# A Mamba block with two feed-forward blocks on one core: state products in halves, sums a tick sooner, carried states in the first factors, four residual additions a unit on GpSimd

## The chip, the core and the metric

The kernel runs on one core of a Trainium2 chip. Its engines are TensorE (PE in the profile; its weight loads PEld), VectorE (DVE), ScalarE (ACT), GpSimd (POOL) and SyncE (SP), which issues nearly all transfers. Each engine works through a queue of its own in order and waits on semaphores for the others. The metric is the device time of one execution in microseconds, as the median over the runs; one further execution is recorded by the hardware profiler.

## The reference

Input `x` is (4, 1024, 256) in fp32. All arithmetic is fp32.

```python
def block(x):
    x = x + attn(layernorm(x))
    return x + ffn(layernorm(x))

def attn(u):                       # Mamba, then a gated MLP, each with an RMS norm
    h = u + mamba(rmsnorm(u, norm1_w))
    xn = rmsnorm(h, norm2_w)
    return h + (silu(xn @ gate_w.T) * (xn @ up_w.T)) @ down_w.T      # 704 wide

def mamba(u):
    z, x, B, C, dt_raw = split(u @ in_proj_w.T)
    dt = softplus(dt_raw @ dt_proj_w.T + dt_proj_b)
    # 8 groups x 32 channels p, each with 32 states n; over the sequence t:
    #   h[t] = exp(dt[t] * A) * h[t-1] + dt[t] * x[t] * B[t];  y[t] = sum_n h[t] * C[t]
    y = scan(x, dt, A, B, C) + x * D_param
    return (y * silu(z)) @ out_proj_w.T

def ffn(x):                        # 1024 wide, with a Walsh-Hadamard transform
    return fwht(silu(x @ W1.T) * (x @ W3.T)) @ W2.T
```

The scan is the large part: 256 channels with 32 states, 4 sequences of 1024 steps.

## The kernel before, in words

**Units.** A unit is half a sequence, T = 512 steps: `c` = 0 the first half (even units), `c` = 1 the second (odd units), eight units in order. Tokens are the free dimension in the scan.

**Quads and ticks.** The 256 x 32 states of a unit are 64 blocks of 128 partitions (32 states for 4 channels) x 512 steps. Four blocks make a quad, 16 quads a unit, 128 in all. A quad takes two ticks, so a unit has 32 and the kernel 256. Quad q belongs to ticks 2q and 2q+1:

- `dma_da` (L693) spreads dt from DRAM over the state partitions into the tile `da` [128, 4, 512] (1 MB); four such buffers (`pda`). `dma_ub` (L698) does the same with dt*x, half a quad at a time (six buffers), `dma_cr` (L711) with C for two quads.
- `exp` (L720) on ScalarE turns `da` into exp(dt*A), two blocks a tick, a quad ahead.
- `times_b` (L740) on VectorE makes `bx` = dt*x*B in PSUM, two blocks a tick; `scan` (L753) runs two scans a tick on VectorE, `da` in place: each step multiplies by `da` and adds `bx`. Where `c` = 1, the initial value is a per-partition operand, the state that the first half left in the tile `carry`.
- `times_c` (L760) on GpSimd, once per quad in the even tick after it, copies the last states of the four blocks to `carry` where `c` = 0, and multiplies the whole quad by C (L768).
- `sum_states` (L772) on TensorE, in the odd tick after that, adds over the states with four matmuls into `py`, over eight quads. Then a buffer of `da` is free. After the eighth quad `y_dx` (L791, VectorE, tick 2q+4) adds x*D, and `y_z` (L798, GpSimd, tick 2q+5) multiplies by silu(z).

**The dense work** is placed in ticks by hand: `at(tick, lane, fn)` puts a function in a list, and the loop at the end (L840 to L876) runs every tick's lanes in a fixed order (PE, ACT, the scan's steps, DVE, POOL0, `times_c`, POOL, `sum_states`, PEend, ACTend, SP, the reads, SPend). That order is each engine's queue; nothing reorders it later. `pre(u, H)` (L324) norms a unit, transposes it and projects it for its scan, which starts at tick H = 32k; `post(u, E, other)` (L590) does out_proj, the MLP and the FFN of a unit after its scan, E = 32k + 32. So during a unit's scan the engines also do the `post` of the unit before, the end of the one before that, and the `pre` of the next.

In `post`, `add_rows` (L296) does a matmul from tokens back to model columns, two row tiles per PSUM tile, and adds the result to the residual tile `hr` on VectorE between the two scans of a tick (L316). It is called for out_proj (tick E+3, addition at E+4), for the MLP's down projection (E+18) and for W2 (E+36, additions at E+38 and E+40). `row_stats` and `hn` on ScalarE, small vectors on GpSimd (L195, L333 and others) and transposes on TensorE make each norm. `gated` (L245) does the two gated projections: TensorE in steps, silu and a PSUM copy `up` on ScalarE, the product on GpSimd (L274).

**SyncE's queue** holds all reads of the scan in the order of the ticks: at an odd tick `dma_da(q+3)`, after the sums of quad q-1 that free its buffer, then `dma_cr(q+2)`; `dma_ub` six ticks ahead.

Of the kernel before, what the change touches and what calls it, by code (L numbers as in the profile page):

```python
# [9 lines left out]
F32 = mybir.dt.float32  # L10
AF = mybir.ActivationFunctionType
ALU = mybir.AluOpType
# [3 lines left out]
P = 128  # L16
# [3 lines left out]
T = 512  # L20
# [7 lines left out]
def tile_block(ctx: ExitStack, tc: tile.TileContext, a, out):  # L28
# [20 lines left out]
    nc = tc.nc  # L49
# [4 lines left out]
    p3 = ctx.enter_context(tc.tile_pool(name="p3", bufs=3))  # L54
# [10 lines left out]
    def dense_psum():  # L65
        return ps_m.tile([P, T], F32, tag="dense", name="dense")
# [14 lines left out]
    us = [{"b": b, "c": c} for b in range(BATCH) for c in range(SEQ // T)]  # L81
# [80 lines left out]
    def row_stats(u, src, ts, centred=True):  # L162

        if 0 in ts:
            u["mv"] = sm.tile([P, 2, TT], F32, tag="mv", name="mv")
        for t in ts:
            junk = p1.tile([P, DM], F32, tag="junk", name="junk")
            nm, ms = u["mv"][:, 0, t : t + 1], u["mv"][:, 1, t : t + 1]
            if centred:
                nc.scalar.activation(  # L170
                    junk, src[:, t, :], AF.Identity, scale=-1.0 / (16 * DM), accum_out=nm
                )
            nc.scalar.activation(  # L173
                junk,
                src[:, t, :],
                AF.Square,
                bias=nm if centred else 0.0,
                scale=1.0 / 16,
                accum_out=ms,
            )  # L180
# [57 lines left out]
    def at(tick, lane, fn, *args):  # L238
        todo[tick][lane].append(partial(fn, *args))

    def run(tick, lane):
        for fn in todo[tick].pop(lane, ()):
            fn()
# [49 lines left out]
        for i in range(1, len(chunks)):  # L293
            at(tick + 3, "POOL", product, i)

    def add_rows(tick, u, lhs, rhs, per_tick, lane="PE"):  # L296

        po = {}

        def pe(t):  # L300
            if t % 2 == 0:
                po[t // 2] = dense_psum().rearrange("p (t d) -> p t d", t=2)
            left, right = lhs(), rhs()
            n = len(left)
            for k in range(n):
                nc.tensor.matmul(  # L306
                    po[t // 2][:, t % 2, :],
                    lhsT=left[k][:, t * P : (t + 1) * P],
                    rhs=right[k],
                    start=(k == 0),  # L310
                    stop=(k == n - 1),
                )

        def add(i):
            hr = u["hr"][:, 2 * i : 2 * i + 2, :]
            nc.vector.tensor_tensor(hr, hr, po[i], ALU.add)  # L316

        for t in range(TT):
            at(tick + t // per_tick, lane, pe, t)
            if t % 2:  # L320
                at(tick + t // per_tick + 1, "DVE", add, t // 2)


    def pre(u, H):  # L324

        s = {}
# [227 lines left out]
        else:  # L554
# [6 lines left out]
            at(H - 31, "ACT", un, (2, 3))  # L561
            at(H - 30, "PE", lambda: transposes(u, s["un"]))
            at(H - 30, "ACTend", transposed, u, "ut")
        at(H - 24, "PE", pe_x)
        at(H - 23, "ACT", act_x)
        at(H - 22, "SP", dma_xb)
        at(H - 19, "SPend", dma_xr, 0)
        at(H - 17, "SPend", dma_xr, 1)
        at(H - 16, "PE", pe_dt)
# [20 lines left out]
    def post(u, E, other):  # L590


        s = {}
# [28 lines left out]
        def store():  # L622
# [11 lines left out]
            lambda: [W["wo"][:, k, :] for k in range(2)],  # L634
            4,
            "PEend",
        )
        at(E + 5, "ACTend", lambda: row_stats(u, u["hr"], (0, 1), False))
        at(E + 6, "ACTend", lambda: row_stats(u, u["hr"], (2, 3), False))
# [26 lines left out]
        for i in range(3):  # L666
# [4 lines left out]
            lambda: [u["g"][:, c, :] for c in range(8)],  # L671
            lambda: [w2h[:, c, :] for c in range(8)],
            1,
        )
        at(E + 43, "SPend", store)

# [3 lines left out]
    qs = [  # L680
        {"u": us[q // 16], "h": q // 8 % 2, "j": q // 2 % 4, "g": q % 2, "n": q % 16}
        for q in range(NQ)
    ]
# [9 lines left out]
    def dma_da(q):  # L693
        s = qs[q]
        s["da"] = pda.tile([P, 4, T], F32, tag="da", name="da")
        spread(s, s["da"], "dtd")
# [35 lines left out]
    def carry_of(s):  # L732
        return s["u"]["carry"][:, s["h"], s["j"], :, s["g"]]
# [19 lines left out]
    def scan(q, b):  # L753
        s = qs[q]
        u = s["u"]
        da = s["da"][:, b, :]
        start = 0.0 if u["c"] == 0 else carry_of(s)[:, b : b + 1]
        nc.vector.tensor_tensor_scan(da, da, s["bx"][:, b % 2, :], start, ALU.mult, ALU.add)  # L758

    def times_c(q):  # L760
        s = qs[q]
        u = s["u"]
        if u["c"] == 0:
            if s["n"] == 0:
                kept = p2.tile([P, 2, 4, 4, 2], F32, tag="carry", name="carry")
                u["carry"] = us[us.index(u) + 1]["carry"] = kept
            nc.gpsimd.tensor_copy(carry_of(s), s["da"][:, :, T - 1])  # L767
        nc.gpsimd.tensor_tensor(  # L768
            s["da"], s["da"], s["cr"].unsqueeze(1).broadcast_to([P, 4, T]), ALU.mult
        )  # L770

    def sum_states(q):  # L772
        s = qs[q]
        u = s["u"]
        first, last = s["n"] % 8 == 0, s["n"] % 8 == 7
        if first:
            u["py"] = ps_y.tile([P, T], F32, tag="y", name="py")
        for b in range(4):
            nc.tensor.matmul(  # L779
                u["py"][32 * b : 32 * b + 32, :],  # L780
                lhsT=rsel[:, 2 * s["j"] + s["g"], :],
                rhs=s["da"][:, b, :],
                start=first,
                stop=last,
            )
        if last:
            at(2 * q + 4, "DVE", y_dx, u, s["h"])
            at(2 * q + 5, "POOL0", y_z, u, s["h"])


    def y_dx(u, h):  # L791
# [10 lines left out]
    for k, u in enumerate(us):  # L802
        pre(u, 32 * k)
    for k, u in enumerate(us):
        post(u, 32 * k + 32, us[k + 2] if k + 2 < len(us) else None)

    def weights_ready():
        nc.scalar.activation(nega, nega, AF.Exp)
# [4 lines left out]
    at(-17, "ACTend", weights_ready)  # L813
    at(-2, "DVE", times_b, 0, 0)
    at(-2, "SP", dma_da, 1)
    at(-1, "SPend", dma_cr, 0)
    at(-1, "SPend", dma_cr, 1)
    loads = [
# [18 lines left out]
    def has(q):  # L837
        return 0 <= q < NQ

    tick = min(todo)  # L840
    while todo:
        q, half = divmod(tick, 2)
        run(tick, "PE")
        run(tick, "ACT")
        if has(q) and tick:
            times_b(q, 2 * half)
        run(tick, "ACTb")
        if has(q + 1):
            for b in (2 * half, 2 * half + 1):
                exp(q + 1, b)  # L850
        if has(q):
            scan(q, 2 * half)
        run(tick, "DVE")
        if has(q):
            scan(q, 2 * half + 1)
        run(tick, "POOL0")
        if half == 0 and has(q - 1):
            times_c(q - 1)
        run(tick, "POOL")
        if half == 1 and has(q - 1):  # L860
            sum_states(q - 1)
        run(tick, "PEend")
        run(tick, "ACTend")
        run(tick, "SP")
        for x in range(2, 6) if tick == -1 else (tick + 6,):
            if tick >= -1 and has(x // 2):
                dma_ub(*divmod(x, 2))
        if half == 1 and q >= -1:
            if has(q + 3):
                dma_da(q + 3)  # L870
            if has(q + 2) and q >= 0:
                dma_cr(q + 2)
        run(tick, "SPend")
        assert not todo[tick], (tick, list(todo[tick]))
        del todo[tick]
        tick += 1  # L876
# [68 lines left out]
```

## Time and profile before

| what | value |
|---|---|
| median of 3 runs | 1173.02 us (1168.52 to 1174.16) |
| the profiled execution's own time | 1170.45 us |
| its span, first to last instruction | 1168.7 us |
| granted TensorE clock, mean | 0.902 |
| VectorE's last `bx` product starts | 1046.98 us |
| first unit with all its `post` neighbours, start of its scan | 411.45 us (the fourth unit) |
| DMA share of 16 engines in units three to seven | 0.86 to 0.90 |
| DMA share in the first unit | 0.94 |

The page gives busy time for each engine, groups of equal instructions with their mean duration and the idle time ahead of them with what ended it, and the waits. A line number is that of the kernel's source; several tiles can share a line, as in `add_rows`. Idle time of an engine matters only where another waits for it: here VectorE has hardly any up to 1050 us and nearly nothing to do after that, when the `post` of the last unit is left.

### The profile page before, as it was taken

The numbers are of one execution on the slowest core, as the hardware profiler recorded it, in microseconds if no ns is written. First come the engines' busy times: TensorE is split into PE (matmuls) and PEld (weight loads), VectorE is DVE, ScalarE is ACT, GpSimd is POOL, SyncE is SP. The second block draws the span as 40 slices with busy tenths as digits, with TensorE's granted clock in tenths as the row PEclk, the third lists the DMA queues.
The fourth block names the chain that finished last, engine by engine and source line by source line (L and its number), as shares of the span: only waits on it lengthen the run. The fifth ranks groups of instructions, "written<-read, shape, count | busy, mean of one in ns | idle before, by whom it ended". The sixth has DMA issues, their size and how long they took to land. (4 is left out here: it accounts for less than half of the span.)

```text
span 1168.7 us, 11833 instructions
## 1 busy us (share of the span) xinstructions
PE 957.9 (82%) x3374; PEld 454.9 (39%) x3374; DVE 975.0 (83%) x860; ACT 772.7 (66%) x1391; POOL 853.5 (73%) x487
## 2 busy tenths in 40 slices
PE   7464246969997899969996999888996987799978
PEld 3121022423633355423633363334542352436535
DVE  5888899999989999999989999999989999991000
ACT  3836565878678786778678776878676847563331
POOL 6675766878878987879878977788786978674212
PEclk9777558979999899979998999979997999799989
DMA  7989998897899889998899889888889789820000
GB/s 250 351 319 365 343 325 294 307 327 285 284 339 325 308 289 337 318 312 284 293 332 323 292 304 342 309 311 296 298 305 342 266 301 322 277 102 2 17 0 19
DMA packets 89443, 321.89 MB, mean 275 GB/s; under 512 B 9313, under 2 KB 20001, under 8 KB 73121
## 3 DMA queue, kind: packets, MB, share of 16 engines
q1 hardware_dynamic: 87520, 318.38, 77.2%
q10 hardware_dynamic: 1856, 2.75, 0.7%
q8 instruction: 27, 0.44, 0.1%
q14 instruction: 40, 0.32, 0.1%
HBM read 302.22 MB, written 18.87 MB: 275 GB/s over the span
## 5 line engine op out<-in xcount | busy, mean ns | idle before, releaser
L768 POOL TENSOR_TENSOR da<-da,cr 128x2048 f32<-128x2048 f32 x128 | 579.9, 4531 | 106.3 <-DVE da L758 24.6
L725 ACT ACTIVATE da<-da,nega 128x512 f32<-128x512 f32 x508 | 333.4, 713 | 170.6 <-DMA da<-dtd 165.0
L749 DVE TENSOR_TENSOR bx<-ub,pb 128x1024 f32<-128x1024 f32 x254 | 312.1, 1229 | 24.1 <-ACT pb L738 12.8
L758 DVE TENSOR_TENSOR_SCAN da<-da,carry,bx 128x512 f32<-128x512 f32 x256 | 316.4, 1269 | 17.8 <-DVE bx L749 6.4
L758 DVE TENSOR_TENSOR_SCAN da<-da,bx 128x512 f32<-128x512 f32 x256 | 300.8, 1210 | 24.1 <-ACT da L725 7.2
L779 PE MATMUL py<-da,rsel 128*32 128x512 f32 x1024 | 161.2, 707 | 169.1 <-POOL da L768 168.8
L226 PE MATMUL dense<-xt,w 128*128 128x512 f32 x512 | 238.5, 621 | 0.0
L226 PEld LDWEIGHTS dense<-xt,w 128*128 128x128 f32 x512 | 99.3, 199 | 144.7 <-issue 124.9
L779 PEld LDWEIGHTS py<-da,rsel 128*32 128x32 f32 x1024 | 21.4, 115 | 253.0 <-POOL da L768 211.1
L316 DVE TENSOR_TENSOR hr<-hr,dense 128x512 f32<-128x512 f32 x48 | 31.6, 669 | 99.6 <-PE dense L306 99.6
L306 PE MATMUL dense<-w2h,g 128*128 128x256 f32 x512 | 113.4, 380 | 0.0
L306 PEld LDWEIGHTS dense<-w2h,g 128*128 128x128 f32 x512 | 96.8, 190 | 18.4 <-ACT junk L173 3.4
L274 POOL TENSOR_TENSOR g<-si,up 128x512 f32<-128x512 f32 x64 | 80.5, 1273 | 27.5 <-ACT up L270 27.4
L306 PE MATMUL dense<-wd,m 128*128 128x256 f32 (+1 forms) x384 | 98.5, 402 | 0.9 <-POOL m L274 0.9
L226 PE MATMUL dense<-ut,win 128*128 128x512 f32 x192 | 97.6, 641 | 1.1 <-ACT ut L220 1.1
L270 ACT COPY up<-dense 128x512 f32<-128x512 f32 x112 | 63.5, 580 | 50.2 <-PE dense L226 50.0
L226 PE MATMUL dense<-ht,wg 128*128 128x512 f32 x192 | 88.3, 603 | 3.3 <-ACT ht L220 3.3
L274 POOL TENSOR_TENSOR m<-si,up 128x512 f32<-128x512 f32 (+1 forms) x48 | 60.2, 1273 | 39.7 <-ACT up L270 39.5
L306 PEld LDWEIGHTS dense<-wd,m 128*128 128x128 f32 (+1 forms) x384 | 68.9, 192 | 37.7 <-issue 23.9
L263 ACT ACTIVATE si<-dense 128x512 f32<-128x512 f32 x112 | 61.0, 595 | 30.8 <-PE dense L226 28.0
L226 PE MATMUL dense<-ht,wu 128*128 128x512 f32 x160 | 72.8, 600 | 1.8 <-ACT si L263 1.7
L767 POOL COPY carry<-da 128x4 f32<-128x4 f32 x64 | 12.1, 189 | 76.2 <-DVE da L758 74.7
(92 smaller groups left out, 785.0 us busy)
## 6 DMA issues: line engine op xcount, KB each, us to landing
da<-dtd SPq DMA_DIRECT2D x127, 1024.0 KB
ub<-ud SPq DMA_DIRECT2D x254, 512.0 KB
cr<-cd SPq DMA_DIRECT2D x64, 256.0 KB
x<-in_x SPq DMA_DIRECT2D x8, 512.0 KB
dtd<-dt SPq DMA_DIRECT2D x16, 256.0 KB
ud<-du SPq DMA_DIRECT2D x16, 256.0 KB
cd<-cc SPq DMA_DIRECT2D x16, 256.0 KB
out<-hr SPq DMA_DIRECT2D x8, 512.0 KB
```

What stands on the lines that cost most here:

```text
L226: nc.tensor.matmul(dst[:n], lhsT=w[:, k, col : col + n], rhs=src[:, k, :], start=(k == 0), stop=(k == 1),)
L263: nc.scalar.activation(g[i]["si"][:n], g[i]["pg"][:n], AF.Silu)
L270: nc.scalar.copy(g[i]["up"][:n], g[i]["pu"][:n])
L274: nc.gpsimd.tensor_tensor(u[dst][:n, c, :], g[i]["si"][:n], g[i]["up"][:n], ALU.mult)
L306: nc.tensor.matmul(po[t // 2][:, t % 2, :], lhsT=left[k][:, t * P : (t + 1) * P], rhs=right[k], start=(k == 0), stop=(k == n - 1),)
L316: nc.vector.tensor_tensor(hr, hr, po[i], ALU.add)
L725: nc.scalar.activation(da, da if q else s["u"]["pdt", b], AF.Exp, scale=an[:, s["h"], s["j"], b, s["g"] : s["g"] + 1],)
L749: nc.vector.tensor_tensor(s["bx"], s["ub", b0 // 2], u["pb"].unsqueeze(1).broadcast_to([P, 2, T]), ALU.mult)
L758: nc.vector.tensor_tensor_scan(da, da, s["bx"][:, b % 2, :], start, ALU.mult, ALU.add)
L767: nc.gpsimd.tensor_copy(carry_of(s), s["da"][:, :, T - 1])
L768: nc.gpsimd.tensor_tensor(s["da"], s["da"], s["cr"].unsqueeze(1).broadcast_to([P, 4, T]), ALU.mult)
L779: nc.tensor.matmul(u["py"][32 * b : 32 * b + 32, :], lhsT=rsel[:, 2 * s["j"] + s["g"], :], rhs=s["da"][:, b, :], start=first, stop=last,)
```

## The change

- `times_c` takes half a quad: two blocks in the tick after their scans, so GpSimd does one 128x1024 product in every tick in place of one 128x2048 in every second, and the carry copy in halves where `c` = 0.
- `sum_states(q-1)` moves from the odd to the even tick, and so do the reads of `da` and `cr` and, by one tick, `y_dx`, `y_z` and the whole of `post` (E = 32k + 31). The first projection of `pre` and its write to DRAM move a tick too, and the third read of `da` is issued at the start.
- Where `c` = 1 the scan starts from the number 1.0. A new step on GpSimd, `start_from`, multiplies the first column of `da` by `carry` a tick before the scan.
- The additions behind out_proj and W2 leave VectorE for all units but the last: ScalarE copies the PSUM tile to an `up` buffer (`evict`), GpSimd adds it (`add_pool`). The addition behind the down projection stays.

```diff
-    def add_rows(tick, u, lhs, rhs, per_tick, lane="PE"):
+    def add_rows(tick, u, lhs, rhs, per_tick, lane="PE", on_pool=False):
...
+        def evict(i):
+            ev = p3.tile([P, T], F32, tag="up", name="ev")
+            po[i] = ev.rearrange("p (t d) -> p t d", t=2), po[i]
+            nc.scalar.copy(*po[i])
+
+        def add_pool(i):
+            hr = u["hr"][:, 2 * i : 2 * i + 2, :]
+            nc.gpsimd.tensor_tensor(hr, hr, po[i][0], ALU.add)
+
         for t in range(TT):
             at(tick + t // per_tick, lane, pe, t)
             if t % 2:
-                at(tick + t // per_tick + 1, "DVE", add, t // 2)
+                after = tick + t // per_tick + 1
+                if on_pool:
+                    at(after, "ACT", evict, t // 2)
+                    at(after, "POOL", add_pool, t // 2)
+                else:
+                    at(after, "DVE", add, t // 2)
...
-        at(H - 24, "PE", pe_x)
-        at(H - 23, "ACT", act_x)
-        at(H - 22, "SP", dma_xb)
+        at(H - 25, "PE", pe_x)
+        at(H - 24, "ACT", act_x)
+        at(H - 23, "SP", dma_xb)
...
             4,
             "PEend",
+            on_pool=u is not us[-1],
...
             lambda: [w2h[:, c, :] for c in range(8)],
             1,
+            on_pool=u is not us[-1],
...
-        start = 0.0 if u["c"] == 0 else carry_of(s)[:, b : b + 1]
+        start = float(u["c"])
         nc.vector.tensor_tensor_scan(da, da, s["bx"][:, b % 2, :], start, ALU.mult, ALU.add)

-    def times_c(q):
+    def start_from(q, half):
+        s = qs[q]
+        if s["u"]["c"]:
+            two = slice(2 * half, 2 * half + 2)
+            first = s["da"][:, two, 0]
+            nc.gpsimd.tensor_tensor(first, first, carry_of(s)[:, two], ALU.mult)
+
+    def times_c(q, half):
         s = qs[q]
         u = s["u"]
+        two = slice(2 * half, 2 * half + 2)
         if u["c"] == 0:
-            if s["n"] == 0:
+            if s["n"] == 0 and half == 0:
...
-            nc.gpsimd.tensor_copy(carry_of(s), s["da"][:, :, T - 1])
+            nc.gpsimd.tensor_copy(carry_of(s)[:, two], s["da"][:, two, T - 1])
         nc.gpsimd.tensor_tensor(
-            s["da"], s["da"], s["cr"].unsqueeze(1).broadcast_to([P, 4, T]), ALU.mult
+            s["da"][:, two, :],
+            s["da"][:, two, :],
+            s["cr"].unsqueeze(1).broadcast_to([P, 2, T]),
+            ALU.mult,
         )
...
-            at(2 * q + 4, "DVE", y_dx, u, s["h"])
-            at(2 * q + 5, "POOL0", y_z, u, s["h"])
+            at(2 * q + 3, "DVE", y_dx, u, s["h"])
+            at(2 * q + 4, "POOL0", y_z, u, s["h"])
...
-        post(u, 32 * k + 32, us[k + 2] if k + 2 < len(us) else None)
+        post(u, 32 * k + 31, us[k + 2] if k + 2 < len(us) else None)
...
+    at(-1, "SPend", dma_da, 2)
...
         run(tick, "POOL0")
+        if has((tick - 1) // 2):
+            times_c(*divmod(tick - 1, 2))
+        if has((tick + 1) // 2):
+            start_from(*divmod(tick + 1, 2))
+        run(tick, "POOL")
         if half == 0 and has(q - 1):
-            times_c(q - 1)
-        run(tick, "POOL")
-        if half == 1 and has(q - 1):
             sum_states(q - 1)
...
-        if half == 1 and q >= -1:
+        if half == 0 and q >= 0:
             if has(q + 3):
                 dma_da(q + 3)
-            if has(q + 2) and q >= 0:
+            if has(q + 2):
                 dma_cr(q + 2)
```

## The prediction

> **What bounds the kernel now.** I read the page first, then busy time by stretches, then the waits, then each engine in order of time inside one unit. T(t) is the start of VectorE's `bx` product in tick t of a unit (t = 0 to 31).
>
> Page, part 1 and the groups (operation, shapes, count; busy us, mean ns; idle before it):
>
> ```profile
> PE 957.9 (82%) x3374; PEld 454.9 (39%) x3374; DVE 975.0 (83%) x860; ACT 772.7 (66%) x1391; POOL 853.5 (73%) x487
> ...
> L768 POOL TENSOR_TENSOR da<-da,cr 128x2048 f32<-128x2048 f32 x128 | 579.9, 4531 | 106.3 <-DVE da L758 24.6
> ...
> L749 DVE TENSOR_TENSOR bx<-ub,pb 128x1024 f32<-128x1024 f32 x254 | 312.1, 1229 | 24.1 <-ACT pb L738 12.8
> L758 DVE TENSOR_TENSOR_SCAN da<-da,carry,bx 128x512 f32<-128x512 f32 x256 | 316.4, 1269 | 17.8 <-DVE bx L749 6.4
> L758 DVE TENSOR_TENSOR_SCAN da<-da,bx 128x512 f32<-128x512 f32 x256 | 300.8, 1210 | 24.1 <-ACT da L725 7.2
> ...
> L316 DVE TENSOR_TENSOR hr<-hr,dense 128x512 f32<-128x512 f32 x48 | 31.6, 669 | 99.6 <-PE dense L306 99.6
> ```
>
> Busy by stretches (length, then PE, PEld, DVE, ACT, POOL with counts, granted clock, DMA share, GB/s): a unit without, a unit with carried states, the tail:
>
> ```profile
> 540.00:666.00 126.00, 113.49 (x415) 54.36 (x414) 118.72 (x104) 96.14 (x176) 105.43 (x64) 0.95 0.87 313
> 666.00:795.00 129.00, 116.01 (x425) 55.22 (x427) 122.76 (x105) 98.15 (x178) 103.76 (x51) 0.95 0.88 313
> ...
> 1050.00:1169.00 119.00, 105.23 (x350) 62.33 (x348) 7.01 (x10) 33.87 (x73) 33.56 (x27) 0.97 0.03 9
> ```
>
> VectorE is 94 to 95% busy in these units and sets the ticks up to 1050 us; after that TensorE alone works. But TensorE (90%) and GpSimd (81 to 84%) are close behind. The waits (us, times, longest):
>
> ```profile
> PE py L779 <- POOL da L768: 168.8, 56, 12.6
> ACT da L725 <- DMA da<-dtd: 165.0, 54, 10.4
> ...
> DVE bx L749 <- ACT pb L738: 12.8, 7, 6.1
> ```
>
> The large ones are not VectorE's: ScalarE's 165 us for reads are hidden, as VectorE waits under 10 us for its exponentials. TensorE in order of time shows where it has no room:
>
> ```profile
> 681.18 3.29 PE L306 MATMUL dense<-wo,yt 128*128 128x256 f32 x14 [0.78 <-POOL yt L799]
> ...
> 706.49 5.42 PE L226 MATMUL dense<-ht,wg 128*128 128x512 f32 x12 [0.51 <-ACT ht L220]
> ...
> 737.12 1.07 PE L779 MATMUL py<-da,rsel 128*32 128x512 f32 x8 [0.24 <-POOL da L768]
> ...
> 742.14 0.72 DVE L794 SCALAR_TENSOR_TENSOR yt<-xr,dpar,py 128x512 f32<-128x512 f32 x1
> ```
>
> From out_proj to the sums at 737.12 it stands still about 1.3 us in 56. Those sums feed the `y_dx` at 742.14, so only some 4 us are spare.
>
> **What the skill says.** GPSIMD Engine Reference, § 3.1: a two-input add of 2048 fp32 takes 4497 ns there, 1.96 times VectorE's; the trace agrees (4531 ns), and has 2366 ns for 128x1024, 1273 for 128x512. § 4.1: GpSimd cannot reach PSUM, so a moved addition needs a ScalarE copy first; no GpSimd row here reads `dense`. SBUF — State Buffer, § Who interferes with whom: a VectorE instruction with at most one SBUF input doesn't contend with GpSimd. `bx` and the scans have one each, and L768 stays between 4500 and 4557 ns all through, so I charge no slowdown for two busy engines. Perfetto Trace Analysis, § GPSIMD Engine Instruction, advises spacing over spans: three 128x512 products in a row span 3.73 us, 1.23 each; a 128x4 step is 0.28 from start to start.
>
> **The change, part by part**, against the profiled execution (1170.5 us, span 1168.7; the median of the runs is 1173.0, 2.6 above it, so the same difference is applied there).
>
> Carried states: 256 scans go from 1269 to 1210 ns: 15.1 us off VectorE. In their place GpSimd runs 128 multiplications of 128x2, absent before; nearest row 128x4, 0.20 us, 0.28 spaced. Bounds: 0.19 (the mean of the carry copies, L767) and 0.35 (an estimate for its strided operands, from the 0.29 that the 128x128 copies of L457 take). I take 0.28.
>
> Residual additions: 28 of 48 leave VectorE (7 units x 4) at 0.669: 18.7 us. ScalarE gains 28 copies of 0.58 (row L270), 16 us on an engine 76% busy, hidden as work. As a queue it is not: the copy stands ahead of `hn` and the exponentials, and waits for TensorE. Out_proj ends near T(3)+5.7; W2 (14.1 us in this trace) and one set of sums (1.1) bring T(3)+20.9, which is T(8)+2.1; then copy 0.6, `hn` 1.7 and two exponentials 1.35: those of tick 7 end near T(9)+2.1, and the scan wants them at T(9)+1.3. Some 0.8 us late, in the place where GpSimd is late too. GpSimd gains 28 x 1.24.
>
> Halves: 4.53 becomes 2 x 2.37, +0.2 a quad; carry copies double, +0.28 a quad in even units. Sums start 2.37 instead of 4.53 us after a scan, 2.2 sooner, but their consumers (`post`, `y_dx`, `y_z`) move a whole tick, 3.75. So the consumers lose 1.6 us of slack. The `da` reads go out some 2 us sooner, with `cr` behind them, and move ahead of `ub`, `xr` and weight loads on SP; each lands ticks before its use, and what it relieves is already hidden. Only the first unit, with DMA 94% busy, may gain: 1 us. `pe_x` and the `xb` write move with it, hidden.
>
> Sum off VectorE: 15.1 + 18.7 = 33.8 us. A tick becomes 3.75 (now 7.49 for two without carry, 7.76 with).
>
> What is late next, first GpSimd. In a carried unit a tick costs 2.37 + 0.09 + 0.28 = 2.74 and leaves 1.0. Extra work per unit is 37 us (14 products, 4 additions, 2 `y_z`, 2 `du` at 1.24 each; the residual with x 2.33; small vectors 7.4). It falls in heaps: products in ticks 1, 2, 11, 12 (two), 14, 15 (two), 27, 28 (two), 30, 31 (two); additions in 3 (two), 5, 7; `y_z` in 2 and 18; `du` in 5 and 19; the residual in 8; small vectors in 6, 22, 25, 27. 32 x 2.74 + 37 = 125 against VectorE's 32 x 3.75 + 2.5 = 122.5: GpSimd no longer fits. The scan of tick t+1 now waits for a multiplication that is queued behind products, additions and the h*C of t-1. Slack: 3.75 + 1.33 to its scan, less 2.37 + 0.37 + 0.1, so 2.25 us. Adding the load tick by tick (each tick gives back 1.0, a lag over 2.25 stalls VectorE): 1.5 us at tick 0, 1.5 at 4, 1.1 over 6 to 8, 1.3 at 9, 0.4 at 16, 1.5 at 29 = 7.3; with overlapping starts (2.61) it is 5.6. I take 6.5 for the fourth and sixth unit, 3 for the second (no W2 before it), 4.5 for the last (no `pre`): 20.5.
>
> Then TensorE in units without carry. Its work from out_proj to the sums of tick 16 stays some 54 us, while `y_dx` comes 3.75 sooner and four additions (2.4) no longer stretch the ticks; 3.4 to 4 us were spare. Short by 2.5 us, three units: 7.5. In carried units the GpSimd stalls cover it.
>
> Tail: sums come about 2.3 us sooner after the last scan. But unit 6's W2 copies now stand ahead of the last unit's `hn` on ScalarE, so the transposes that followed W2 at once wait for copy 0.6 and `hn` 1.7: 2.2 back. Zero.
>
> Total: -33.8 + 20.5 + 7.5 - 1 = -7 (-6.8), so 1166 on the median. Own range -14 to -1: 1159 to 1172.
>
> **Rivals.**
> Full gain: GpSimd and TensorE absorb it, since VectorE is the busiest and GpSimd shows 22 us idle a unit. Against it is the 125 against 122.5. At best 34 less: 1139; more likely, partly, 1139 to 1158.
> Slower: GpSimd becomes the pacemaker. One mechanism: the first-factor multiplication sits in its queue behind work that itself waits for ScalarE's copies, and the next h*C, sums and reads follow late. Place: the carried units. Price: each 0.1 us more a tick costs 3.2 us a unit. To lose the 6.8 it takes 2 us in each of 3.5 such units, 0.06 a tick; for slower by 0.5%, 3.6 us, 0.11 a tick. The 0.35 bound of the small multiplication brings 0.07, the late exponentials 1 us a unit. With 5 us: 1183. For it: in the unit read GpSimd was never late by more than 0.8 us, with a spare that is now gone. Against: even units let it catch up.
> No effect: each shift is eaten exactly by a loop TensorE closes, about 127 us a unit now and then: 1173. Here the sooner reads and sums are a transfer hidden anyway.
> That the halves don't act is unlikely: in the order of the changed kernel's instructions the first and third sum matmul of a quad wait for GpSimd separately.
>
> **How the numbers follow.** Likeliest 0.50, full or half gain 0.17, slower 0.25, no effect 0.08. A difference of 0.5% (5.9 us) is about what a measurement of this kernel tells from none. Of the likeliest, 0.29 lies beyond it: faster 0.46, same 0.29, slower 0.25. Range: it leaves under a tenth of the full gain below 1149 and about a tenth above 1185.
>
> **What would show it.** Scans all near 1.21 us; 20 `hr` rows left on VectorE; GpSimd at 93 to 98% in carried units and VectorE waiting for its 128x2 rows at ticks 0, 4, 9 and 29; `y_dx` waiting for sums in even units; `hn` later in the tail. Wrong if VectorE shows no such waits and units take 123 us (full gain), or if units with carry exceed 131 us.

## The result, and the profile after

The changed kernel takes 1187.03 us (median of 4 runs, 1183.99 to 1188.73), the kernel before in the same series 1173.59 us (1168.52 to 1174.52). The ratio is 1.012, with a 95% interval of 1.008 to 1.016: slower by 1.2%, where 1166 was forecast. The profiled execution took 1183.99 us with a span of 1182.1.

From the page after, part 1 and the groups (operation, shapes, count; busy us, mean ns; idle before it and what ended most of that):

```profile
PE 1018.1 (86%) x3374; PEld 468.8 (40%) x3374; DVE 942.8 (80%) x832; ACT 787.3 (67%) x1419; POOL 936.2 (79%) x835
...
L775 DVE TENSOR_TENSOR_SCAN da<-da,bx 128x512 f32<-128x512 f32 x512 | 600.1, 1209 | 71.8 <-POOL da L782 26.2
L793 POOL TENSOR_TENSOR da<-da,cr 128x1024 f32<-128x1024 f32 x256 | 603.4, 2357 | 59.3 <-DVE da L775 21.9
...
L807 PE MATMUL py<-da,rsel 128*32 128x512 f32 x1024 | 222.7, 678 | 130.2 <-POOL da L793 128.0
```

VectorE did lose its work: 975.0 us became 942.8, which is the forecast of 33.8 within 2, and all scans take 1209 ns. But the span grew by 13.4 us. The line that was not foreseen is that of the sums: the same 1024 matmuls keep TensorE busy for 222.7 us now, and for 161.2 in the page before:

```profile
L779 PE MATMUL py<-da,rsel 128*32 128x512 f32 x1024 | 161.2, 707 | 169.1 <-POOL da L768 168.8
```

The waits of after (us, times, longest):

```profile
PE py L807 <- POOL da L793: 128.0, 55, 9.9
...
ACT ev L321 <- PE dense L306: 95.5, 28, 6.8
ACT da L741 <- DMA da<-dtd: 60.3, 19, 9.9
...
DVE bx L765 <- ACT pb L754: 28.7, 7, 5.6
DVE da L775 <- POOL da L782: 26.2, 19, 3.8
```

ScalarE's hidden wait for reads fell from 165.0 to 60.3 us, and no gain followed. VectorE waits for the 128x2 multiplications (26.2 us, `POOL da L782`) and, more than before (12.8), for the copy of B into PSUM (28.7, `ACT pb L754`).

The time is lost in one half of each unit. From one `y_dx` of VectorE to the next a unit falls into two stretches, tick 1 to 17 and tick 17 to 33. Where the consumers keep their old ticks, as in the kernel before, the same `y_dx` lie a tick later (2, 18 and 34). The first row is the mean over units three to seven, the second over units two to seven:

| stretch | before | after |
|---|---|---|
| tick 1 to tick 17 | 64.9 us | 69.6 us |
| tick 17 to tick 33 | 62.8 us | 62.2 us |
| last `bx` of the kernel | 1046.98 us | 1061.06 us |
| from there to the end of the span | 121.7 us | 121.0 us |

Five units at 4.7 us more in the first are some 24 us; the shorter second stretches, and the second and the last unit (62.8 and 63.9 us in the first stretch), give some 10 back. Units with and without carried states lose alike: 69.8 and 69.8 us, then 69.2 and 69.3. This speaks against the carried states, and against anything else that only one kind of unit has, as the cause. TensorE in order of time, at the start of the fifth unit, one without carried states (ticks 1 to 3; start, length, what it is, in brackets the wait):

```profile
551.73 1.05 PE L807 MATMUL py<-da,rsel 128*32 128x512 f32 x4
556.69 1.85 PE L807 MATMUL py<-da,rsel 128*32 128x512 f32 x4 [3.90 <-POOL da L793]
558.47 4.57 PE L306 MATMUL dense<-wo,yt 128*128 128x256 f32 x16
562.88 7.07 PE L306 MATMUL dense<-w2h,g 128*128 128x256 f32 x32
```

Out_proj (L306, `wo,yt`) is queued behind the sums of its tick. The first half of these sums runs at once; the second then stands for 3.90 us until GpSimd has multiplied the second half of the quad by C, and then takes 1.85 us where the first took 1.05. GpSimd at the same time:

```profile
551.55 1.29 POOL L274 TENSOR_TENSOR g<-si,up 128x512 f32<-128x512 f32 x1
552.78 1.30 POOL L827 TENSOR_TENSOR yt<-yt,zs 128x512 f32<-128x512 f32 x1
...
554.29 2.35 POOL L793 TENSOR_TENSOR da<-da,cr 128x1024 f32<-128x1024 f32 x1
```

The input of out_proj, `y_z` (L827), was ready at 554.08. Out_proj started at 558.47, 4.4 us later, and only because of what stood ahead of it in TensorE's queue. The granted clock in the same microseconds (length, then PE, PEld, DVE, ACT, POOL busy, granted clock, DMA share, GB/s):

```profile
550.00:555.00 5.00, 2.65 (x16) 0.99 (x12) 4.88 (x6) 5.00 (x10) 4.92 (x5) 1.00 0.83 292
555.00:560.00 5.00, 3.31 (x8) 1.40 (x9) 4.83 (x6) 2.32 (x5) 4.92 (x4) 0.68 0.78 274
```

The stand lowered TensorE's clock to 0.68 on the mean of 5 us. The longest gap ahead of out_proj is 3.6 to 3.9 us for the out_proj of each of the second to the seventh unit in the changed kernel (it runs at the start of the unit that follows); before, it was 0.8 to 2.7. In the kernel before, the sums stand between two shorter waits at this place:

```profile
552.43 1.06 PE L779 MATMUL py<-da,rsel 128*32 128x512 f32 x8 [1.40 <-POOL da L768]
553.42 0.70 PE L306 MATMUL dense<-wo,yt 128*128 128x256 f32 x2
554.89 3.29 PE L306 MATMUL dense<-wo,yt 128*128 128x256 f32 x14 [0.77 <-POOL yt L799]
```

The Trainium skill has a rule for this in "TensorE: Matmul & The Clock Gate", Part 1: The HAM clock gate: TensorE's clock is halved after an idle window of some 3.4 us, whose start is not tied to the kernel, and is released after about as long a time of work. The traces agree on the halving (single out_proj matmuls take 379 ns at the median and 796 at most) and on the window: in each of the 19 traces here, all changes of the granted clock lie on a grid of 3.41 us. They do not agree that the window must be idle. By the profile's busy times, TensorE was busy for less than 46% of 428 windows at full clock, and the clock fell after 420 of these; it was busy for longer in 4883, and the clock fell after 12. As an estimate from these numbers, 1.84 us of standing in one window (54% of 3.41) can be enough, and a stand of twice that, 3.7 us, is enough wherever the grid falls. Here the measurement decides.

From out_proj on TensorE works in units three to seven of both kernels without a pause over 0.6 us as far as the sums of tick 16 (in the changed kernel the second half of those waits another 2.0 to 2.35 us for h*C). Whatever VectorE wants of that chain comes late as well, in whichever queue it is waited for:

```profile
700.25 2.33 DVE L775 TENSOR_TENSOR_SCAN da<-da,bx 128x512 f32<-128x512 f32 x2 [3.32 <-POOL da L782]
...
745.90 1.23 DVE L765 TENSOR_TENSOR bx<-ub,pb 128x1024 f32<-128x1024 f32 x1 [2.70 <-ACT pb L754]
```

Both are from a unit with carried states. The first, at tick 5, reads like a late GpSimd. But GpSimd had itself stood 2.11 and 0.46 us at its two additions, for ScalarE's copies of out_proj, of which the first had stood 5.09 us for TensorE. The second, at tick 16, stands behind `up` copies on ScalarE, the first of which waits 1.17 us for TensorE.

### The profile page after: what moved, and what is told of

Read it like the earlier page. It is cut to its first block, busy times and chain, and to the rows that moved or that the text cites. A ratio compares the mean times of both kernels' runs of the same rounds, so it can differ in the third digit from the quotient of the medians.

```text
span 1182.1 us, 12287 instructions
## 1 busy us (share of the span) xinstructions
PE 1018.1 (86%) x3374; PEld 468.8 (40%) x3374; DVE 942.8 (80%) x832; ACT 787.3 (67%) x1419; POOL 936.2 (79%) x835
## 5 line engine op out<-in xcount | busy, mean ns | idle before, releaser
L775 DVE TENSOR_TENSOR_SCAN da<-da,bx 128x512 f32<-128x512 f32 x512 | 600.1, 1209 | 71.8 <-POOL da L782 26.2
L793 POOL TENSOR_TENSOR da<-da,cr 128x1024 f32<-128x1024 f32 x256 | 603.4, 2357 | 59.3 <-DVE da L775 21.9
L741 ACT ACTIVATE da<-da,nega 128x512 f32<-128x512 f32 x508 | 331.3, 713 | 67.6 <-DMA da<-dtd 60.3
L765 DVE TENSOR_TENSOR bx<-ub,pb 128x1024 f32<-128x1024 f32 x254 | 312.1, 1229 | 39.6 <-ACT pb L754 28.7
L807 PE MATMUL py<-da,rsel 128*32 128x512 f32 x1024 | 222.7, 678 | 130.2 <-POOL da L793 128.0
L226 PE MATMUL dense<-xt,w 128*128 128x512 f32 x512 | 229.2, 602 | 0.0
L807 PEld LDWEIGHTS py<-da,rsel 128*32 128x32 f32 x1024 | 29.2, 113 | 265.3 <-POOL da L793 208.1
L306 PE MATMUL dense<-w2h,g 128*128 128x256 f32 x512 | 113.4, 380 | 0.0
L306 PE MATMUL dense<-wd,m 128*128 128x256 f32 (+1 forms) x384 | 104.9, 421 | 0.9 <-POOL m L274 0.9
L306 PEld LDWEIGHTS dense<-w2h,g 128*128 128x128 f32 x512 | 96.8, 190 | 18.4 <-ACT ev L321 5.0
L316 DVE TENSOR_TENSOR hr<-hr,dense 128x512 f32<-128x512 f32 x20 | 13.4, 672 | 101.9 <-PE dense L306 101.9
L274 POOL TENSOR_TENSOR m<-si,up 128x512 f32<-128x512 f32 (+1 forms) x48 | 60.3, 1271 | 42.7 <-ACT up L270 42.7
L306 PEld LDWEIGHTS dense<-wd,m 128*128 128x128 f32 (+1 forms) x384 | 73.1, 203 | 40.6 <-issue 24.3
L263 ACT ACTIVATE si<-dense 128x512 f32<-128x512 f32 x112 | 62.8, 596 | 37.0 <-PE dense L226 36.1
L321 ACT COPY ev<-dense 128x512 f32<-128x512 f32 x28 | 16.4, 586 | 95.5 <-PE dense L306 95.5
L325 POOL TENSOR_TENSOR hr<-hr,ev 128x512 f32<-128x512 f32 x28 | 35.6, 1271 | 31.3 <-ACT ev L321 30.8
```

The source lines that it names most:

```text
L226: nc.tensor.matmul(dst[:n], lhsT=w[:, k, col : col + n], rhs=src[:, k, :], start=(k == 0), stop=(k == 1),)
L263: nc.scalar.activation(g[i]["si"][:n], g[i]["pg"][:n], AF.Silu)
L274: nc.gpsimd.tensor_tensor(u[dst][:n, c, :], g[i]["si"][:n], g[i]["up"][:n], ALU.mult)
L306: nc.tensor.matmul(po[t // 2][:, t % 2, :], lhsT=left[k][:, t * P : (t + 1) * P], rhs=right[k], start=(k == 0), stop=(k == n - 1),)
L321: nc.scalar.copy(*po[i])
L325: nc.gpsimd.tensor_tensor(hr, hr, po[i][0], ALU.add)
```

## The experiments

Each kernel was timed beside the kernel before on the same chip. Medians of the kernel before were 1171.2 to 1172.4 us in these series. "Stretch" below is tick 1 to 17, as above.

**Which part of the change: four undone one at a time, or reordered.**

`adds_back`: both `on_pool=u is not us[-1]` removed.

> The changed kernel with the 28 residual additions back on VectorE (no ScalarE copies, no GpSimd additions); the rest of the change stays. Theory A (TensorE's chain: from out_proj to the up copies of the second MLP group it runs without a pause, its start is not sooner than before, and the copy of B into PSUM at tick 15 stands behind it): the additions fall into VectorE's own idle time before tick 16, so units without carry stay near 130 us; carried units win 2 to 3 us from a lighter GpSimd: 1178 to 1184 us. Theory B (GpSimd is the pacemaker): 5 us less of its work per unit, stalls at the 128x2 rows mostly gone, 1168 to 1176 us. Theory C (the ScalarE copies that wait for TensorE hold up the exponentials and hn): 1164 to 1170 us, waits for exponentials back under 10 us.

Measured: 1187.45 us, ratio 1.0135 (1.0114 to 1.0156), stretch 69.5. The difference from the changed kernel is within the spread of the runs, so the 28 additions are worth nothing here, in either direction: the waits for the 128x2 rows fell from 26.2 to 6.5 us, and the additions themselves wait for TensorE some 23 us more than in the changed kernel. Theories B and C fall; the time lies 3 us above theory A's range too, as the 2 to 3 us for carried units did not come.

`post_back`:

```diff
-        post(u, 32 * k + 31, us[k + 2] if k + 2 < len(us) else None)
+        post(u, 32 * k + 32, us[k + 2] if k + 2 < len(us) else None)
...
-            at(2 * q + 3, "DVE", y_dx, u, s["h"])
-            at(2 * q + 4, "POOL0", y_z, u, s["h"])
+            at(2 * q + 4, "DVE", y_dx, u, s["h"])
+            at(2 * q + 5, "POOL0", y_z, u, s["h"])
```

and `pe_x`, `act_x`, `dma_xb` a tick later, as before.

> The changed kernel with everything behind the sums (y_dx, y_z, out_proj, MLP, FFN, pe_x) a tick later again, where it was before; halves, sooner sums and reads, carried states in first factors and GpSimd additions stay. Theory A: the copy of B at tick 15 stands ahead of the ups of its own tick again, units without carry fall from 131 to about 127 us, carried ones from 132.5 to about 130: 1160 to 1170 us. Theory B (GpSimd): its load is the same, 1181 to 1190 us. Theory C (ScalarE copies): same load and same order behind TensorE, 1180 to 1190 us.

Measured: 1169.71 us, ratio 0.9981 (0.9973 to 0.9988), stretch 67.6. The sooner consumers are what makes the changed kernel slow; with them a tick later the gap ahead of out_proj is 0.7 to 1.5 us for units two to seven. The waits for the copy of B did not go, though (35.1 us), so theory A's detail on them was wrong.

`carry_back`: `start = 0.0 if u["c"] == 0 else carry_of(s)[:, b : b + 1]`, and no `start_from`.

> The changed kernel with the carried state as the scan's initial operand again (no 128x2 multiplications); the rest of the change stays. Theory A: units without carry stay at 130 to 131 us; carried ones lose 26 us of waits for the 128x2 rows in all and gain 15 us of scan time, part of which the other waits take: 1176 to 1186 us. Theory B: with the multiplication gone GpSimd's lateness no longer reaches VectorE, 1172 to 1177 us, and units without carry shorten too. Theory C: no change, 1182 to 1190 us.

Measured: 1190.92 us, ratio 1.0161 (1.0133 to 1.0189), stretch 69.7. The 26 us of waits for the 128x2 rows are gone with those rows, the scans take their 15 us more again, and the kernel is no faster. So these waits do not explain the loss: as a cost of their own they would have left some 11 us of gain. The median lies above the range of each of the three theories.

`out_first`:

```diff
-            "PEend",
+            "PE0",
             on_pool=u is not us[-1],
...
         run(tick, "POOL")
+        run(tick, "PE0")
         if half == 0 and has(q - 1):
             sum_states(q - 1)
```

> The changed kernel with one order changed: out_proj is queued on TensorE ahead of the sums of its tick instead of behind them. Theory A: out_proj no longer waits for the second half of h*C (3.90 us in the seventh unit's start), the chain to tick 16 starts 3 to 4 us sooner, units without carry lose 3 to 4 us each, carried ones 1 to 3: 1168 to 1178 us. Theory B and theory C: 1184 to 1190 us, no change.

Measured: 1162.40 us, ratio 0.9922 (0.9905 to 0.9939), stretch 65.4. One order on one queue brings some 24 us, more than expected. TensorE at the start of the same unit as above (the fifth, which the expectation calls the seventh):

```profile
543.72 0.60 PE L306 MATMUL dense<-wo,yt 128*128 128x256 f32 x2
546.15 3.29 PE L306 MATMUL dense<-wo,yt 128*128 128x256 f32 x14 [1.84 <-POOL yt L827]
549.38 1.06 PE L807 MATMUL py<-da,rsel 128*32 128x512 f32 x8
```

Out_proj waits 1.84 us, keeps the full clock, and the sums behind it find both halves ready. Of its waits, those for the 128x2 rows are down to little more than half, though GpSimd's work is the same (us, times, longest):

```profile
DVE bx L765 <- ACT pb L754: 26.9, 7, 5.3
...
DVE da L775 <- POOL da L782: 14.2, 16, 1.6
```

**The late start or the lower clock: `warm`.** Idle multiplications fill the stand; no order is changed.

```diff
+            if b == 1 and s["n"] == 0 and u is not us[0]:
+                warm = dense_psum()
+                for _ in range(3):
+                    nc.tensor.matmul(warm, lhsT=ident, rhs=w2h[:, 0:2, :], start=True, stop=True)
```

> The changed kernel with three idle multiplications by the identity (nothing reads them, 2.6 us of TensorE work) between the first and the second half of the sums of a unit's first quad, where TensorE stands 3.90 us; no order is changed. Theory D (the stand itself lowers the granted clock, so that the sums after it take 1.85 and out_proj 4.57 us where they take 1.05 and 3.9 at full clock): the clock stays at 1.00 there, 1.5 to 2 us a unit come back, 10 to 14 us in all: 1173 to 1179 us. If only the late start of out_proj counts: 1184 to 1190 us.

Measured: 1173.13 us, ratio 1.0003 (0.9992 to 1.0014), stretch 67.4. TensorE at the start of the same unit:

```profile
549.58 1.05 PE L807 MATMUL py<-da,rsel 128*32 128x512 f32 x4
550.56 2.84 PE L817 MATMUL dense<-w2h,ident 128*128 128x512 f32 x6
554.57 1.05 PE L807 MATMUL py<-da,rsel 128*32 128x512 f32 x4 [1.16 <-POOL da L793]
555.55 3.72 PE L306 MATMUL dense<-wo,yt 128*128 128x256 f32 x16
```

Work that nobody reads makes the kernel 14 us faster. For all of units two to seven the gap is 1.0 to 1.2 us and out_proj takes 3.72 instead of 4.6 to 5.8. Of the 24 us between the changed kernel and `out_first`, 14 are thus the clock that the stand lowers. The other 10 come with the order. In units three to seven out_proj ends 12.5 to 13.7 us after `y_dx` in the changed kernel, 10.8 in `warm` and 6.8 to 7.1 in `out_first`; that this earlier place brings the 10 us is argued, as no run has it with the clock still low.

**Does the place of the copy of B matter: `pb_sooner`.** In the second MLP group all `up` copies and products go to tick + 3, `up` in a lane behind the copy of B and the exponentials.

> The changed kernel with the three ups and three products of the second MLP group moved behind the copy of B and the exponentials of tick 15 (ScalarE no longer waits for TensorE ahead of that copy); all else stays. Theory A1 (the place of this copy in ScalarE's queue is what holds VectorE): the waits for it fall from 28.7 us (7 of them) to under 8, the stretch from tick 1 to tick 17 from 69.6 to about 66, the run to 1165 to 1175 us. Theory A2 (TensorE's chain itself holds VectorE, whichever product of it is waited for): the waits for the copy go, and return at the exponentials, whose da buffers wait for the sums, or at y_dx of tick 17: 1180 to 1190 us.

Measured: 1192.56 us, ratio 1.0167 (1.0124 to 1.0211), stretch 70.1. Theory A1 falls, and the time is above theory A2's range too. The waits for the copy went from 28.7 to 12.5 us, and came back as waits for the 128x2 rows (35.2) and for the sums that `y_dx` wants (18.3, in the changed kernel 7.0). The wait named by the profile was the messenger.

**Are the sums in two pieces a cost: `late_first`.** `for b in range(4)` in `sum_states` becomes `for b in (2, 3, 0, 1)`.

> The changed kernel with the sums of a quad in the order 2, 3, 0, 1, so that the first of them waits for the second half of h*C and the four run together (the first half of h*C still runs early). Theory A3 (the sums in two pieces hold TensorE longer: 1.05 us for the first two of a quad, then a wait, then 1.69 to 1.85 for the other two, where all four together take 1.06): TensorE's busy time falls from 1018 by about 50 us back to 960 to 975; out_proj of tick 2 starts 0.7 us sooner, 5 to 8 us in all: 1178 to 1183 us. If only the moment of the second half matters: 1185 to 1189 us.

Measured: 1198.62 us, ratio 1.0226 (1.0202 to 1.0251). TensorE's busy time fell to 979.0 us, near the forecast of 960 to 975, and the kernel became 11.6 us slower than the changed one: the forecast had the wrong sign.

```profile
563.93 1.94 PE L807 MATMUL py<-da,rsel 128*32 128x512 f32 x8 [4.84 <-POOL da L793]
565.80 4.91 PE L306 MATMUL dense<-wo,yt 128*128 128x256 f32 x16
```

The stand in one piece is longer (4.84 us), and all eight records pay for it. Ahead of out_proj this evens out (stretch 69.3, against 69.6); the loss lies in ticks 17 to 33, 63.7 us against 62.2. Some 20 us after the `y_dx` of tick 17 the clock is halved for 13.7 us in each of units three to eight, in the changed kernel for 6.8 or 10.2, and the copy of B is waited for 13 times instead of 7. That the first pieces of the sums keep the clock up there fits this, but was not tried by itself.

**Would the order have helped the kernel before: `before_out_first`** (the edit of `out_first` on the kernel before) **and `before_out_first_warm`** (with three idle multiplications ahead of out_proj).

> The kernel before with out_proj queued on TensorE ahead of the sums of its tick, nothing else. Theory A: out_proj waits there 1.40 us for h*C and then 0.77 for y_z; it starts when y_z is done, and the sums (1.06) follow: 0.5 to 1.5 us a unit, of which VectorE, 94% busy, takes a part: 1166 to 1172 us. If VectorE sets the ticks of the kernel before: 1170 to 1175 us.

> The kernel before with out_proj ahead of the sums of its tick, and three idle multiplications by the identity (2.6 us) ahead of out_proj, where TensorE stands 3.35 us for y_z in the run without them. Theory D (what that order cost, 13 us, is the clock lowered by an unbroken stand): 1170 to 1177 us, clock 1.00 there, out_proj's second part 3.3 instead of 4.96 us. If the 13 us have another cause: 1183 to 1188 us.

Measured: 1185.47 us, ratio 1.0120 (1.0091 to 1.0149), against the expectation, and 1175.57 us, ratio 1.0037 (1.0025 to 1.0049). TensorE in `before_out_first`, then in the one with idle multiplications:

```profile
560.07 4.96 PE L306 MATMUL dense<-wo,yt 128*128 128x256 f32 x14 [3.35 <-POOL yt L799]
564.96 1.07 PE L779 MATMUL py<-da,rsel 128*32 128x512 f32 x8
```

```profile
550.00 2.84 PE L304 MATMUL dense<-w2h,ident 128*128 128x512 f32 x6 [0.49 <-ACT up L270]
...
553.99 3.29 PE L310 MATMUL dense<-wo,yt 128*128 128x256 f32 x14 [0.71 <-POOL yt L803]
```

In the kernel before, the sums stood between two waits and broke the stand. With out_proj in front there is one wait for `y_z`, 2.3 to 4.3 us for units two to seven, and the clock falls there in five of the six. With the gap filled, 10 of the 13 us come back. The same order costs time in one kernel and brings time in the other, by what it does to the stand.

**Which part makes the stand: `shift_only`** (changed kernel without first factors and with the additions on VectorE) **and `halves_only`** (that, with the consumers at their old ticks).

> The changed kernel without the first-factor multiplications (carry as the scan's operand) and with all additions on VectorE: what remains is halves, sooner sums and reads, and the consumers a tick sooner. Theory A with D (out_proj a tick sooner falls behind sums that wait for the second half of h*C; the stand and the lower clock follow): the stand of 3 to 4 us ahead of out_proj is there without any added GpSimd load, the stretch from tick 1 to tick 17 is 68 to 70 us: 1186 to 1194 us. If GpSimd's added work makes the stand: at most 1 to 2 us of it, 1170 to 1177 us.

> The kernel before with halves of h*C and sooner sums and reads alone: consumers where they were, carry as the scan's operand, additions on VectorE. Theory A with D (the harm is in the sooner consumers): no stand ahead of out_proj, 1169 to 1177 us, so that the sooner consumers cost about 20 us (1195.8 with them). If the halves themselves hurt (GpSimd 0.2 us more a quad, sums in two pieces on TensorE): 1180 to 1195 us. Against the changed kernel with its consumers back (1169.7 us) it gives what carried states and additions are worth without a stand: 2 to 8 us.

Measured: 1195.83 us, ratio 1.0203 (1.0185 to 1.0220), just above the range of theory A with D, and 1175.83 us, ratio 1.0027 (1.0016 to 1.0037), inside it. TensorE in `shift_only`:

```profile
563.66 1.92 PE L805 MATMUL py<-da,rsel 128*32 128x512 f32 x4 [3.86 <-POOL da L791]
565.51 5.32 PE L306 MATMUL dense<-wo,yt 128*128 128x256 f32 x16
```

The stand is there in full without any load that carried states and additions put on GpSimd; in `halves_only` the gap is 0.8 to 1.5 us. So the change comes apart into halves with sooner sums and reads (3 to 4 us slower than the kernel before), the consumers a tick sooner (20 us slower), and carried states and additions together (8.8 us faster on top of that; 6.1 us faster with the consumers at their old ticks, 1175.83 to 1169.71).

**What the parts are worth without the stand, and a better version.** All have the order of `out_first`. To it come: the additions back on VectorE (`out_first_adds_back`); the carry operand back (`out_first_carry_back`); `y_z` a tick sooner, in a lane ahead of GpSimd's products (`out_yz`); the edits of `pb_sooner` and `late_first` (`all_three`); those of `out_yz` and `pb_sooner` (`out_yz_pb`); and these with the additions back (`out_yz_pb_adds_back`):

> Out_proj ahead of the sums of its tick, and the 28 residual additions back on VectorE. If the stretch from tick 1 to tick 17 is still TensorE's (65.4 us), the 18.7 us fall into VectorE's idle time: 1160 to 1166 us as with out_proj first alone. If the prediction's price of the additions holds once the stand is gone: 1170 to 1181 us.

> Out_proj ahead of the sums of its tick, and the carried state as the scan's operand again. By the prediction's sum (15.1 us less VectorE time, about 20 us of waits for the 128x2 rows, of which carried units pay some 17): 1155 to 1165 us, no loss. If GpSimd's lateness is hidden by TensorE's: 1162 to 1170 us. If the 15.1 us are won in full: 1174 to 1178 us.

> Out_proj ahead of the sums of its tick, and y_z ahead of GpSimd's products of the tick of y_dx (a place earlier by one 128x512 product, 1.25 us, and by one 128x1024). Theory A: out_proj waits 1.84 us for y_z now; it starts 1.2 to 1.8 us sooner in six units: 1150 to 1158 us. If TensorE's chain no longer sets that stretch: 1160 to 1164 us.

> The changed kernel with all three orders together: out_proj ahead of the sums of its tick, ups and products of the second MLP group behind the copy of B and the exponentials, sums in the order 2, 3, 0, 1. Theory A: each takes something off the stretch from tick 1 to tick 17 (65.7 us with out_proj first alone), down to 63 to 64; the 128x2 multiplications remain: 1142 to 1158 us. Theory A2: the chain still holds that stretch, 1158 to 1165 us. Theory B: GpSimd at its limit, 1160 to 1170 us.

> Out_proj ahead of the sums of its tick, y_z ahead of GpSimd's products, and the ups and products of the second MLP group behind the copy of B and the exponentials. Theory A1 (without the stand, this copy's place in ScalarE's queue is what is left of TensorE's hold on VectorE; it is waited for 26.2 us): 1142 to 1154 us. Theory A2 (the hold moves to the sums that y_dx of tick 17 wants): 1157 to 1163 us. It may be slower, as this move alone was in the changed kernel: up to 1168 us.

> The same with the 28 additions back on VectorE. Theory A1: VectorE has no idle time left for them, 10 to 18 us slower than with them on GpSimd: 1156 to 1168 us. Theory A2: no difference, or a little faster, as ScalarE's queue has no copies that wait for TensorE: 1154 to 1163 us.

| kernel | us | ratio to before (95% interval) | stretch |
|---|---|---|---|
| out_first | 1162.40 | 0.9922 (0.9905 to 0.9939) | 65.4 |
| out_first_adds_back | 1161.51 | 0.9902 (0.9874 to 0.9929) | 65.6 |
| out_first_carry_back | 1173.49 | 1.0005 (0.9990 to 1.0020) | 65.8 |
| out_yz | 1161.08 | 0.9905 (0.9871 to 0.9938) | 65.4 |
| all_three | 1176.06 | 1.0040 (1.0024 to 1.0056) | 66.3 |
| out_yz_pb | 1164.91 | 0.9949 (0.9932 to 0.9966) | 65.7 |
| out_yz_pb_adds_back | 1158.11 | 0.9887 (0.9872 to 0.9903) | 64.7 |

The carried states bring 11.1 us once the stand is gone (9.7 by the ratios). The additions bring nothing on GpSimd, and cost 6.8 us in the pair of `out_yz_pb`. `all_three` lies above all three ranges of its expectation; it has the order of `late_first` in it, which cost 11.6 us by itself and probably takes back most of the gain here. `y_z` 1.3 us sooner was not felt. The edit of `pb_sooner` brought nothing with the additions on GpSimd: `out_yz_pb` is 4 us slower than `out_yz`. `out_yz_pb_adds_back` is the fastest, 1.1% below the kernel before. Its stretch of 64.7 us is still above 60.7, which 16 ticks of 3.75 us and a `y_dx` would take; what holds the last 4 us was not found.

## Why the prediction was wrong

- **"A tick becomes 3.75", 33.8 us off VectorE: right.** Busy time fell by 32.2 us, and undisturbed ticks are 3.7 to 3.8 us.
- **The step that failed is "Then TensorE in units without carry", 7.5 us: "Its work from out_proj to the sums of tick 16 stays some 54 us", and "In carried units the GpSimd stalls cover it".** The place was right, and out_proj's own place was nearly right for a full clock: the prediction has "Out_proj ends near T(3)+5.7", and in units three to seven of `warm` it ends at T(3)+5.2 to 5.3. But the wait ahead of it was priced at its length alone, and the work behind it was held constant. In the changed kernel it ends there at T(3)+6.9 to 8.1, as the stand of 3.9 us halves the clock for it and for the sums ahead of it. From its end to the end of the sums of tick 16 it takes 55.6 to 56.6 us, before 53.2 to 53.8: sums in two pieces keep TensorE busy for 1.0 to 1.7 us more there, and the second piece of tick 16 waits 2.0 to 2.35 us. The text has the reason for both waits in it, sums "2.2 sooner" and consumers "a whole tick, 3.75", but booked the 1.6 us between them as lost slack. Carried units lose as much as the others, so nothing was covered. Price: 20 us for the sooner consumers (17 with carried states and additions, against `post_back`) instead of 7.5.
- **The granted clock was left out.** In the trace before, sums take 1.94 us instead of 1.06 after a stand of 5.0 to 5.2 us in each of units two to seven. The prediction priced all TensorE work at the rate of a running chain. 14 of the 17 us come back in `warm`, where the stand is filled. The mean of the clock would not have told this: it is 0.902 before and 0.913 after. What counts is where it is low: in units three to seven before, once a unit and in the second stretch; after, also behind the stand.
- **GpSimd's lag, 20.5 us: near in size (26.2 us), in part right in place, wrong in cause.** In the fourth and sixth unit VectorE waited for the 128x2 rows at ticks 1, 5, 10, 13, 14 and 30, together 10.5 and 10.0 us. Ticks 1, 5 and 30 are the forecast 0, 4 and 29 a tick later; 10, 13 and 14 were not forecast, and 6 to 9 and 16 all but stayed away. GpSimd was busy for 115.7 of 132 us in the sixth unit, 88%, not 125 us and not 93 to 98%. The largest wait, at tick 5, followed from the late out_proj by way of the additions: without the stand 14.2 us of these waits are left, with the additions back as well 8.5. So the near size is luck. The rival "GpSimd becomes the pacemaker" had the right side and nearly the right number (1183), by a mechanism that the runs refute: less load on GpSimd changed nothing (`adds_back`, `carry_back`).
- **Signs.** "Units with carry exceed 131 us" was named as a sign of being wrong, and it came: 133.2 and 132.7 us. `y_dx` waiting for sums in even units did not (0.25 us at most up to the last unit): VectorE was held ahead of it, at the copy of B for tick 16.
- **Carried states: mis-sized against them.** 15.1 us off the scans less their waits was to be a small loss; with the order mended it is a gain of 10 to 11. In the changed kernel the gain is 3.9 us, and the runs of the two kernels overlap.
- **Residual additions, 18.7 us: not earned.** They stood in the stretch in which VectorE waits for TensorE anyway. "ScalarE gains 28 copies ... hidden as work. As a queue it is not" was right: VectorE waits 19.8 us for exponentials in the changed kernel and 8.0 in `adds_back`, and moving the additions back costs nothing or gains.
- **Halves: a cost was missing.** `halves_only` is 3 to 4 us slower than the kernel before, not 1 us faster. That this is the longer work of TensorE on split sums (last section) is likely, but no run shows it alone.
- **Tail, 0 us: right**, 121.7 us before and 121.0 after, and by the two parts that were named: the last `y_dx` comes 2.7 us sooner, and TensorE then waits 1.1 us for `hn`, which stands behind the W2 copies, and transposes at the pace of its rows (1.96 us instead of 1.04).

## What to carry to other kernels

When work is moved to an earlier slot, ask of each engine what stands ahead of it in the queue there and when that is ready, not only when its own inputs are: here out_proj's input was there 4.4 us before out_proj started. A wait on TensorE has two prices: its length and, when it leaves TensorE busy for less than some 46% of one 3.41 us window, half speed for what follows. Here 1.84 us were enough in some units, and 3.6 us in all. Put enough work into the wait, or change the queue's order so that it ends sooner. A mean clock doesn't show this; look at the clock where the chain has no room. And when an engine waits in new places under other names, follow each wait back to its start before blaming the engine that is named.

## What was not expected of the hardware

- **Idle work made the kernel faster**: 2.84 us of multiplications that nothing reads, once a unit, brought 14 us in one kernel and 10 in another.
- **A wait well under 3.4 us can halve the clock.** With out_proj ahead of its sums and a wait of 1.8 to 2.6 us for `y_z`, the clock fell there in one of the six units in `out_first`, in four in `out_first_adds_back`, and in three each in `out_first_carry_back` and `all_three`, for 3.4 us each time. The same wait of 1.84 us left 14 out_proj matmuls at 3.29 us in `out_first` and at 4.88 in one unit of `all_three`. With `y_z` sooner (`out_yz`, waits of 0.5 to 1.7 us) it fell in none. This is what a window fixed in time, less than about half busy, would give; the differences of a few us between these kernels contain it.
- **Sums in two pieces take TensorE twice as long.** At full clock two of a quad's four sums take 1.05 us and all four together 1.06 (`x4` and `x8` in the traces): each goes to its own 32 columns of the array and they run side by side. The Trainium skill says so in "TensorE: Matmul & The Clock Gate", Part 3: Packing small matmuls; the trace puts the price of splitting at 1.05 us a quad wherever the second half comes later. This is most of the 61.5 us by which the line of the sums grew: with the pieces joined (`late_first`) it is at 168.3 us, and yet that kernel was slower.
